# Scan loads and zero fills issued by ScalarE, delta writes by GpSimd, other buffer counts in the scan

## The chip, the cores and the metric

The kernel runs on one core of a Trainium2 chip. The metric is the time of one execution on the device in microseconds; a lower time is better. PE is the matrix engine (TensorE), PEld its weight loads, DVE VectorE, ACT ScalarE, POOL GpSimd, and SP is SyncE, which computes nothing and issues transfers (DMAs).

## The reference

Eight sequences (batches) of 512 steps with 256 channels pass through a chain with residual additions. Shortened to what the text below needs:

```
# 1. gated conditioning, then a Mamba layer
cond  = gated, causally averaged x (nine exponential averages), normalised
xc, z = split(cond @ W_in);  xc = silu(causal_conv4(xc) + conv_b)
dt, B, C = split(xc @ W_x);  delta = softplus(dt @ W_dt + b_dt);  A = -exp(A_raw)
h[t]  = exp(delta[t] * A) * h[t-1] + delta[t] * B[t] * xc[t]     # 16 states x 512 channels
y[t]  = sum_n C[t, n] * h[t, n] + D * xc[t]
x     = x + (y * silu(z)) @ W_out
# 2. per-batch linear layer, then 2 of 8 experts for each token (gelu), x = x + sum
# 3. per-batch low-rank feed-forward layer, then attention, 8 heads, 512 x 512 scores:
a     = softmax(q k^T);  x = x + sum over heads (a @ V)
# 4. per-batch bottleneck and layer norm, then 4 of 32 experts for each token, shared expert
```

## The kernel before

The work on the batches is written as two Python generators that are stepped in turn, so that their instructions lie mixed in the program. A scheduler then orders the instructions of each engine: it takes them by program order, but lets a later one that is ready pass an earlier one that is not. On the chip each engine works through its own queue in that order and stops at a wait.

**Thread X** (`thread_x`) does part 1 for batches 0 to 7. `head_a` computes the conditioning, with scans over time on DVE (line 479). `head_b` does the input projection, the convolution of four taps (lines 523 to 533: ACT writes the padded copy `xp` and the first tap, DVE adds three), silu, and delta (lines 557 to 574). What the scan needs goes through DRAM: `xzs` holds xc and silu(z), `packs` holds delta and delta * xc, because each block of 32 channels is read back repeated four times onto 128 partitions, one copy for each of four states. `scan` then works through 64 items (j, g, k) of a batch: j is a group of 128 channels, g a group of four states, k a block of 32 channels. `begin(i)` makes dA on ACT (line 623, the scaled Exp) and h on POOL (line 625); `run(i)` makes the recurrence on DVE (line 651) and the product with C (line 652); `add` sums over the states on PE (line 660), and adds D * xc on DVE (line 664) and multiplies with silu(z) on POOL (line 665). `begin` runs two items ahead of `run`. The same block `packed` serves the four g of a j, so a block is loaded (`get_pack`, line 595) for every four items, 128 times in all; its tiles are a ring of five, `dA` one of four, `h` one of eight. While batch b is scanned, the head of batch b+1 is stepped between the items; what is left of it is run before item 58.

**Thread Y** (`thread_y`) does parts 2 and 3 for groups of batches ([0], [1, 2], [3, 4, 5], [6, 7]) as soon as thread X has finished them: routing, scattering tokens into tables in DRAM (`tab`, `tok`) by indirect transfers of POOL (line 160), experts (loads `fw` and `xt`), then low-rank feed-forward and attention. In attention `scores` takes the maximum on DVE (line 893), Exp with its sum on ACT (line 896), the reciprocal on DVE (line 897) and the scaling with it on DVE (line 898); `turn` transposes on PE (line 906). Some copies out of PSUM are written with `nc.any`, and the scheduler gives them to ACT or DVE. Group [6, 7] runs when thread X is over, together with the routing of part 4; the 32 experts come last.

All plain transfers are issued by SP, in one queue for both threads; POOL issues only the indirect ones.

The tables have to be zero before tokens are scattered into them. `filling` steps thread X and, at every fourth of its pieces, issues one fill from a block of zeros, 56 in all of about 2 MB, and ties it to the DVE instruction written last (line 153):

```python
to, src = fills.pop(0)
tc.add_manual_dep(nc.sync.dma_start(to, src).ins, last_of(mybir.EngineType.DVE).name, SYNC)
```

Of the kernel before, what the change touches and what calls it, by code (L numbers as in the profile page):

```python
# [10 lines left out]
F32 = mybir.dt.float32  # L11
I32 = mybir.dt.int32
AF = mybir.ActivationFunctionType
ALU = mybir.AluOpType
# [3 lines left out]
P = 128  # L18
NB = 8
T = 512  # L20
# [31 lines left out]
def adaln_attn_ffn_kernel(ctx: ExitStack, tc: tile.TileContext, d: dict, out: bass.AP):  # L52
    nc = tc.nc
# [84 lines left out]
            fills.append((v[i], zeros[:, 0 : 16 * w]))  # L138
        return t

    def last_of(engine):
        return next(i for i in reversed(nc.cur_bb.bb.instructions) if i.engine == engine)

    def filling(pieces):

        first = E2 * len(GROUPS[0]) * T // (16 * P)
        z = const.tile([P, 132], F32, tag="z", name="z")
        nc.vector.memset(z, 0.0)
        nc.sync.dma_start(zeros.rearrange("p (r f) -> p r f", f=132), z[:, None, :].to_broadcast([P, 32, 132]))
        for n, c in enumerate(pieces):  # L150
            if fills and n % 4 == 1 and (n > 44 or n < 4 * first):
                to, src = fills.pop(0)
                tc.add_manual_dep(nc.sync.dma_start(to, src).ins, last_of(mybir.EngineType.DVE).name, SYNC)
            yield c

    members = {}
# [210 lines left out]
    def thread_x(wp, wk, ps):  # L367
# [63 lines left out]
                nc.vector.scalar_tensor_tensor(  # L431
                    cb[:, j : j + 1], wb[:, j : j + 1], col("convw", 4 * j + 3), col("convb", j), ALU.mult, ALU.add)

        xps = []
        for i in range(2):
            t = wp.tile([P, T + 3], F32, tag=f"xp{i}", name=f"xp{i}")
            nc.gpsimd.memset(t[:, 0:3], 0.0)
            xps.append(t)
        m3 = wp.tile([72, T], BF16, tag="m3", name="m3")
        nc.gpsimd.memset(m3, 0.0)  # L440

# [77 lines left out]
        def head_b(b):  # L519

            cn = rows[b]
            xc = wk.tile([P, 4, T], F32, tag="xc", name="xc")
            for j in range(4):
                pt = gx()
                mm(pt, [(W_in[:, k, ts(j, P)], cn[:, k, :]) for k in range(KC)])
                xp = xps[j % 2]
                nc.scalar.activation(xp[:, 3:], pt, AF.Identity, bias=wb[:, j : j + 1])
                cv = xc[:, j, :]
                nc.scalar.activation(cv, pt, AF.Identity, scale=col("convw", 4 * j + 3), bias=cb[:, j : j + 1])
                for i in range(3):  # L530
                    nc.vector.scalar_tensor_tensor(
                        cv, xp[:, i : i + T], col("convw", 4 * j + i), cv, ALU.mult, ALU.add)
                yield 3
            nc.scalar.activation(xc, xc, AF.Silu)
            nc.sync.dma_start(xzs[b % 2][:, :, 0, :], xc)
            for j in range(4):
                pt = gx()
                mm(pt, [(W_in[:, k, ts(4 + j, P)], cn[:, k, :]) for k in range(KC)])
                sz = wk.tile([P, T], F32, tag="sg", name="sz", bufs=2)
                nc.scalar.activation(sz, pt, AF.Silu, bias=wb[:, 4 + j : 5 + j])  # L540
                nc.sync.dma_start(xzs[b % 2][:, j, 1, :], sz)
            yield 5
            pt = gx()
            mm(pt[:96, :], [(W_x[:, j, :], xc[:, j, :]) for j in range(4)])
            dt = wk.tile([64, T], F32, tag="dt", name="dt")
            nc.scalar.copy(dt, pt[:64, :])
            bc3 = wk.tile([96, T], BF16, tag="bc3", name="bc3", bufs=2)
            split3(wk, pt[64:96, :], [bc3[64:96, :], bc3[32:64, :], bc3[0:32, :]], 64, 96)
            yield 3

            for j2 in range(2):
                dds, es = [], []
                for j in (2 * j2, 2 * j2 + 1):
                    pt = gx()
                    mm(pt, [(W_dt[:, ts(j, P)], dt)])

                    dd = wk.tile([P, 2, T], F32, tag=("gated", "ct")[j % 2], name="dd")
                    e = wk.tile([P, T], F32, tag="sg", name="sp_e", bufs=2)
                    nc.scalar.activation(e, pt, AF.Abs, bias=col("bdt", j))
                    nc.vector.tensor_scalar(dd[:, 0, :], pt, col("bdt", j), 0.0, ALU.add, ALU.max)  # L560
                    nc.scalar.activation(e, e, AF.Exp, scale=-1.0)
                    u = dd[:, 1, :]
                    nc.vector.tensor_scalar(u, e, 1.0, None, ALU.add)
                    nc.vector.scalar_tensor_tensor(e, u, 1.0, e, ALU.subtract, ALU.subtract)
                    dds.append(dd)
                    es.append(e)
                yield 3
                for dd in dds:
                    nc.scalar.activation(dd[:, 1, :], dd[:, 1, :], AF.Ln)
                for j, dd, e in zip((2 * j2, 2 * j2 + 1), dds, es):  # L570
                    u = dd[:, 1, :]
                    nc.gpsimd.tensor_tensor(u, u, e, ALU.subtract)
                    nc.gpsimd.tensor_tensor(dd[:, 0, :], dd[:, 0, :], u, ALU.add)
                    nc.gpsimd.tensor_tensor(dd[:, 1, :], dd[:, 0, :], xc[:, j, :], ALU.mult)
                    nc.sync.dma_start(packs[b % 2][j], dd)
                yield 3
            rows[b] = bc3

# [11 lines left out]

        def get_pack(b, j, k):

            t = wk.tile([P, 2, T], F32, tag="pack", name="packed", bufs=5)
            src = packs[b % 2][j, 32 * k : 32 * k + 32]
            nc.sync.dma_start(t, src[None].to_broadcast([4, 32, 2, T]))
            got[b, j, k] = t

        def get_B4(b, g):

            pt = gx()  # L600
            mm(pt, [(states(g), rows[b])])
            t = wk.tile([P, T], F32, tag="B4", name="B4", bufs=4)
            nc.scalar.copy(t, pt)
            B4s[b, g] = t
# [7 lines left out]
        def scan(b):  # L612
# [6 lines left out]
            def begin(i):  # L619
                j, g, k = items[i]  # L620
                t = got[b, j, k]
                dA = wk.tile([P, T], F32, tag="dA", name="dA", bufs=4)
                nc.scalar.activation(dA, t[:, 0, :], AF.Exp, scale=A[:, 4 * j + k, g : g + 1])  # L623
                h = wk.tile([P, T], F32, tag="h", name="h", bufs=8)
                nc.gpsimd.tensor_tensor(h, t[:, 1, :], B4s[b, g], ALU.mult)  # L625
                hs[i], dAs[i] = h, dA
                if (g, k) == (1, 0):
                    xz[j] = wk.tile([P, 2, T], F32, tag="xz", name="xz")
                    nc.sync.dma_start(xz[j], xzs[b % 2][:, j])
                if j == 0 and g < 3 and k == 1:  # L630
                    get_B4(b, g + 1)

                if j < 3 and (g, k) == (2, 3):
                    get_pack(b, j + 1, 0)
                if j < 3 and g == 3 and k < 3:
                    get_pack(b, j + 1, k + 1)
                if j == 3 and b + 1 < NB and g == 3:
                    if k == 0:
                        get_pack(b + 1, 0, 0)
                    if k < 3:  # L640
                        get_pack(b + 1, 0, k + 1)
                    if k == 3:
                        get_B4(b + 1, 0)

            def run(i):
                j, g, k = items[i]
# [20 lines left out]
            begin(0)  # L667
            begin(1)
            for i in range(64):
                if i == 58:  # L670
                    yield from after[0]
                if i < 62:
                    begin(i + 2)
                run(i)
                if i % 4 == 0 and i > 0:
                    add(i - 4)
                if i % 2:
                    yield 5
# [32 lines left out]
    def thread_y(q, bs, ps):  # L711
# [103 lines left out]
        with ExitStack() as ph:  # L815
            wk = ph.enter_context(tc.tile_pool(name=f"k3_{q}", bufs=1))
            H = 8
            for r, b in enumerate(bs):
# [43 lines left out]
                for hp in range(H // 2):  # L862
# [20 lines left out]
                    def scores(i):  # L883

                        sps = [g() for u in range(2)]

                        for u in (1, 0):
                            r0 = 64 * u
                            mm(sps[u], [(qk[r0 : r0 + 64, 0, ts(i, P)], qk[r0 : r0 + 64, 1, :])])
                        for u in range(2):  # L890
                            sp = sps[u]
                            nm = wk.tile([P, 1], F32, tag="nm", name="nm", bufs=4)
                            nc.vector.tensor_reduce(nm, sp, AX.X, ALU.max, negate=True)  # L893
                            ex = wk.tile([P, T], F32, tag="ex", name="ex", bufs=NEX)
                            den = wk.tile([P, 1], F32, tag="den", name="den", bufs=4)
                            nc.scalar.activation(ex, sp, AF.Exp, bias=nm, accum_out=den)  # L896
                            nc.vector.reciprocal(den, den)
                            nc.vector.tensor_scalar(ex, ex, den, None, ALU.mult)  # L898
                            exs[i, u] = ex

                    def turn(i):
# [300 lines left out]
```

## Time and profile before

| | before |
|---|---|
| median of 3 runs | 4261.57 us (4254.47 to 4265.86) |
| profiled execution | 4252.41 us, span from first to last instruction 4250.6 us |
| PE busy | 3440.5 us, 81% |
| DVE busy | 2670.9 us, 63% |
| ACT busy | 1672.2 us, 39% |
| POOL busy | 1565.8 us, 37% |
| transfers | 554.78 MB, mean 131 GB/s |
| granted PE clock, mean | 0.889 |

The profile is of one execution. Busy time counts no transfer issues. A line such as "POOL h L625 <- DMA packed<-pack: 190.2, 47, 16.1" says that POOL, ahead of the instruction of line 625 that writes h, sat idle until a transfer from `pack` into `packed` had landed: 190.2 us in total, 47 times, 16.1 us at the longest. SPq is the queue in which SP issues transfers. A line of the timeline has start, duration, engine, line and operation, and in brackets the idle time before it with what ended it. Shares over the whole span hide that the stages have different limits, so tables by stretch of time are used as well.

### The profile page before, as it was taken

The page shows a single profiled execution, that of the slowest core. Times are in us where ns is not written, and L with a number is a line of the kernel's source. Part 1 is how long each engine was busy: PE and PEld are TensorE (multiplying, and loading weights), DVE is VectorE, ACT ScalarE, POOL GpSimd, SP SyncE. Part 2 cuts the span into 40 slices and gives each one's busy share as a digit, 9 for nine tenths or more (in the row PEclk, how much of TensorE's full clock was granted, in tenths as well). Part 3 has the DMA queues.
Part 4 walks back from the last instruction along what each step waited for, and adds up shares of the span by engine and source line. Part 5 has one row for each costly group of instructions (what it writes and reads, how often), then busy time and mean ns, then how long its engine had stood idle before and what let it go on. Part 6 is the DMA issues. An engine that isn't in the chain of part 4 may idle for free. (4 is left out here: it accounts for less than half of the span.)

```text
span 4250.6 us, 36891 instructions
## 1 busy us (share of the span) xinstructions
PE 3440.5 (81%) x10964; PEld 1694.3 (40%) x10964; DVE 2670.9 (63%) x4290; ACT 1672.2 (39%) x2741; POOL 1565.8 (37%) x1222
## 2 busy tenths in 40 slices
PE   4556686887687888888758899889988999978994
PEld 2111352332254233333327443333456444436773
DVE  4698957886966686796892547575432454443336
ACT  2535463455366346445433443242223233322222
POOL 0456535434635333433542323231043111134552
PEclk7677798988798898999879999899989999989996
DMA  3235455324456423333346312213043312117776
GB/s 105 101 108 180 187 162 170 106 98 156 177 176 209 135 102 118 134 122 109 139 165 234 122 63 77 68 36 104 15 163 136 93 41 70 36 50 245 248 237 224
DMA packets 159372, 554.78 MB, mean 131 GB/s; under 512 B 27730, under 2 KB 34289, under 8 KB 146756
## 3 DMA queue, kind: packets, MB, share of 16 engines
q1 hardware_dynamic: 135076, 501.35, 35.2%
q0 software_dynamic: 24096, 51.08, 3.3%
q8 instruction: 87, 1.43, 0.1%
q14 instruction: 113, 0.93, 0.1%
HBM read 453.00 MB, written 234.82 MB: 162 GB/s over the span
## 5 line engine op out<-in xcount | busy, mean ns | idle before, releaser
L625 POOL TENSOR_TENSOR h<-packed,B 128x512 f32<-128x512 f32 x512 | 792.5, 1570 | 1054.2 <-PE yp L660 746.7
L651 DVE TENSOR_TENSOR_SCAN h<-dA,h 128x512 f32<-128x512 f32 x512 | 791.0, 1571 | 126.3 <-ACT dA L623 67.2
L623 ACT ACTIVATE dA<-packed,Aexp 128x512 f32<-128x512 f32 x512 | 359.8, 720 | 656.4 <-DVE h L651 446.5
L160 POOL DMA_INDIRECT tok<-ys,to_i x310 | 311.9, 1006 | 497.9 <-DVE ys L808 237.7
L660 PE MATMUL yp<-h,fold 128*32 128x512 f32 x1024 | 349.7, 704 | 156.9 <-DVE h L652 140.6
L923 PE MATMUL acc<-aT,V 128*128 128x512 f32 x1024 | 453.4, 597 | 5.3 <-ACT aT L907 3.2
L160 POOL DMA_INDIRECT tab<-row,si x192 | 197.4, 1028 | 465.5 <-issue 210.5
L652 DVE TENSOR_TENSOR h<-h,c 128x512 f32<-128x512 f32 x512 | 330.5, 672 | 29.0 <-PE c L78 28.2
L923 PEld LDWEIGHTS acc<-aT,V 128*128 128x128 f32 x1024 | 193.2, 191 | 245.9 <-issue 235.1
L78 PE MATMUL acc<-wv,c 128*128 128x512 f32 x512 | 270.2, 642 | 0.4
L78 PE MATMUL g<-qk 64*128 64x512 f32 x512 | 210.7, 681 | 54.9 <-ACT ex L896 28.6
L896 ACT ACTIVATE ex<-g,nm 128x512 f32<-128x512 f32 x256 | 173.8, 684 | 157.5 <-DVE nm L893 157.3
L78 PE MATMUL g<-xT,fw 128*128 128x256 f32 x960 | 233.6, 396 | 2.5 <-ACT h L801 1.9
L893 DVE TENSOR_REDUCE nm<-g 128x1 f32<-128x512 f32 x256 | 165.0, 681 | 100.8 <-PE g L78 100.8
L78 PE MATMUL acc<-fw,h 128*128 128x256 f32 x960 | 221.6, 383 | 3.5 <-DVE ys L808 1.8
L78 PEld LDWEIGHTS g<-xT,fw 128*128 128x128 f32 x960 | 188.0, 201 | 39.4 <-issue 6.8
L78 PEld LDWEIGHTS acc<-fw,h 128*128 128x128 f32 x960 | 182.7, 192 | 41.6 <-issue 12.4
L906 PE MATMUL acc<-ident,ex 128*128 128x128 f32 x1024 | 160.3, 286 | 47.9 <-DVE ex L898 16.2
L906 PEld LDWEIGHTS acc<-ident,ex 128*128 128x128 f32 x1024 | 122.6, 146 | 188.4 <-issue 69.3
L660 PEld LDWEIGHTS yp<-h,fold 128*32 128x32 f32 x1024 | 44.7, 115 | 364.1 <-DVE h L652 208.3
L479 DVE TENSOR_TENSOR_SCAN tr<-alpha,gm 128x512 f32<-128x512 f32 x128 | 181.4, 1435 | 5.0 <-POOL y L665 3.5
L78 PE MATMUL g<-xT,mw 128*128 128x256 f32 x760 | 183.1, 385 | 0.0
(280 smaller groups left out, 5458.3 us busy)
## 6 DMA issues: line engine op xcount, KB each, us to landing
fw<-in_fW SPq DMA_DIRECT2D x60, 1154.0 KB
tab<-zeros SPq DMA_DIRECT2D x32, 2112.0 KB
packed<-pack SPq DMA_DIRECT2D x128, 512.0 KB
mw<-in_mW SPq DMA_DIRECT2D x95, 384.0 KB
tab<-zeros SPq DMA_DIRECT2D x16, 2080.0 KB
xt<-tab SPq DMA_DIRECT2D x95, 264.0 KB
xz<-xzs SPq DMA_DIRECT2D x32, 512.0 KB
pack<-dd SPq DMA_DIRECT2D x32, 512.0 KB
```

Of the source, the lines that this page charges most:

```text
L78: nc.tensor.matmul(o, lhsT, rhs, start=(i == 0), stop=(i == len(pairs) - 1))
L160: i = nc.gpsimd.indirect_dma_start(out=table_, out_offset=bass.IndirectOffsetOnAxis(ap=idx, axis=0), in_=src, in_offset=None, bounds_check ...
L479: nc.vector.tensor_tensor_scan(tr, alpha[:, 1 + i : 2 + i].to_broadcast([P, T]), gm[:, k, :], 0.0, ALU.mult, ALU.add)
L623: nc.scalar.activation(dA, t[:, 0, :], AF.Exp, scale=A[:, 4 * j + k, g : g + 1])
L625: nc.gpsimd.tensor_tensor(h, t[:, 1, :], B4s[b, g], ALU.mult)
L651: nc.vector.tensor_tensor_scan(h, dAs.pop(i), h, 0.0, ALU.mult, ALU.add)
L652: nc.vector.tensor_tensor(h, h, Cs[0], ALU.mult)
L660: nc.tensor.matmul(yps[j][32 * k : 32 * k + 32, :], fold, hs.pop(i + k), start=(g == 0), stop=(g == 3))
L893: nc.vector.tensor_reduce(nm, sp, AX.X, ALU.max, negate=True)
L896: nc.scalar.activation(ex, sp, AF.Exp, bias=nm, accum_out=den)
L906: nc.tensor.transpose(tp[:, m, :], ex[:, ts(m, P)], ident)
L923: nc.tensor.matmul(ys[k], V[:, m, C * u + P * k : C * u + P * (k + 1)], aTs[u][:, m, :], start=(u == 0 and m == 0), stop=(u == 1 and m == 3))
```

## The change

Five things change together:

- The fills are issued by ScalarE, and the dependency on DVE's last instruction is gone.
- In thread X, the writes of xc and silu(z) to `xzs`, the loads of `xz` and the loads of the scan's blocks are issued by ScalarE; the writes of delta to `packs` by GpSimd.
- Six buffers for the blocks in place of five, three for `dA` in place of four, one padded copy `xp` in place of two. The loads of the next j are asked for at (g, k) = (2, 2), (2, 3), (3, 2) and (3, 3), before at (2, 3), (3, 0), (3, 1) and (3, 2).
- What is left of the next head is run before item 56 instead of 58.
- In attention the scaling of the exponentials is a ScalarE activation instead of a DVE operation.

```diff
-                tc.add_manual_dep(nc.sync.dma_start(to, src).ins, last_of(mybir.EngineType.DVE).name, SYNC)
+                nc.scalar.dma_start(to, src)
...
-        xps = []
-        for i in range(2):
-            t = wp.tile([P, T + 3], F32, tag=f"xp{i}", name=f"xp{i}")
-            nc.gpsimd.memset(t[:, 0:3], 0.0)
-            xps.append(t)
+        xp = wp.tile([P, T + 3], F32, tag="xp", name="xp")
+        nc.gpsimd.memset(xp[:, 0:3], 0.0)
...
-            nc.sync.dma_start(xzs[b % 2][:, :, 0, :], xc)
+            nc.scalar.dma_start(xzs[b % 2][:, :, 0, :], xc)
...
-                nc.sync.dma_start(xzs[b % 2][:, j, 1, :], sz)
+                nc.scalar.dma_start(xzs[b % 2][:, j, 1, :], sz)
...
-                    nc.sync.dma_start(packs[b % 2][j], dd)
+                    nc.gpsimd.dma_start(packs[b % 2][j], dd)
...
-            t = wk.tile([P, 2, T], F32, tag="pack", name="packed", bufs=5)
+            t = wk.tile([P, 2, T], F32, tag="pack", name="packed", bufs=6)
             src = packs[b % 2][j, 32 * k : 32 * k + 32]
-            nc.sync.dma_start(t, src[None].to_broadcast([4, 32, 2, T]))
+            nc.scalar.dma_start(t, src[None].to_broadcast([4, 32, 2, T]))
...
-                dA = wk.tile([P, T], F32, tag="dA", name="dA", bufs=4)
+                dA = wk.tile([P, T], F32, tag="dA", name="dA", bufs=3)
...
-                    nc.sync.dma_start(xz[j], xzs[b % 2][:, j])
+                    nc.scalar.dma_start(xz[j], xzs[b % 2][:, j])
...
-                if j < 3 and (g, k) == (2, 3):
-                    get_pack(b, j + 1, 0)
-                if j < 3 and g == 3 and k < 3:
-                    get_pack(b, j + 1, k + 1)
-                if j == 3 and b + 1 < NB and g == 3:
-                    if k == 0:
-                        get_pack(b + 1, 0, 0)
-                    if k < 3:
-                        get_pack(b + 1, 0, k + 1)
-                    if k == 3:
-                        get_B4(b + 1, 0)
+                if g == 2 and k > 1:
+                    block(j + 1, k - 2)
+                if g == 3 and k > 1:
+                    block(j + 1, k)
+                if j == 3 and g == 3 and k == 3 and b + 1 < NB:
+                    get_B4(b + 1, 0)
+
+            def block(j, k):
+                if j < 4:
+                    get_pack(b, j, k)
+                elif b + 1 < NB:
+                    get_pack(b + 1, 0, k)
...
-                if i == 58:
+                if i == 56:
                     yield from after[0]
...
-                            nc.vector.tensor_scalar(ex, ex, den, None, ALU.mult)
+                            nc.scalar.activation(ex, ex, AF.Identity, scale=den)
```

More of the change, by code (lines that the diff above doesn't have):

```diff
@@ L139, in table @@
         return t
-    def last_of(engine):
-        return next(i for i in reversed(nc.cur_bb.bb.instructions) if i.engine == engine)
     def filling(pieces):
@@ L525, in head_b @@
                 mm(pt, [(W_in[:, k, ts(j, P)], cn[:, k, :]) for k in range(KC)])
-                xp = xps[j % 2]
                 nc.scalar.activation(xp[:, 3:], pt, AF.Identity, bias=wb[:, j : j + 1])
```

## The prediction

> **What bounds the kernel now.** I read the stages first (busy time by stretch), then who waits for whom, then the waits of SP's transfer queue, and last the timeline of the start. Columns of the stages: length, busy us (instructions) of PE, PEld, DVE, ACT, POOL, then PE clock, transfer share, GB/s.
>
> ```profile
> 0.00:480.00 480.00, 273.29 (x515) 78.27 (x515) 360.04 (x409) 194.04 (x251) 217.89 (x149) 0.71 0.37 124
> 480.00:2950.00 2470.00, 2031.01 (x6239) 936.27 (x6239) 1747.43 (x2372) 1120.29 (x1789) 977.54 (x698) 0.90 0.39 132
> 2950.00:3810.00 860.00, 800.73 (x2617) 417.77 (x2616) 374.72 (x917) 249.19 (x479) 173.72 (x172) 0.96 0.23 78
> 3810.00:4180.00 370.00, 313.60 (x1532) 252.74 (x1530) 136.04 (x481) 92.42 (x191) 196.60 (x204) 0.96 0.70 222
> 4180.00:4250.00 70.00, 21.84 (x64) 9.26 (x64) 52.65 (x112) 16.27 (x32) 0.00 (x0) 0.50 0.81 300
> ```
>
> To 480 us only thread X runs (batch 0's head, its scan, batch 1's head); DVE is busy 75% and no thread-Y work covers a gap, so a stall there moves the end one for one. From 480 to 2950 X and Y share the engines: PE 82%, DVE 71%, neither full, both losing time to each other. After 2950 the scan is over and PE is 93% busy. The change can act before 2950, and on the softmax after it.
>
> ```profile
> POOL h L625 <- DMA packed<-pack: 190.2, 47, 16.1
> ACT dA L623 <- DMA packed<-pack: 132.2, 38, 7.7
> DVE h L651 <- ACT dA L623: 67.2, 19, 10.8
> DVE h L651 <- POOL h L625: 59.0, 22, 8.6
> DVE dd L560 <- DMA pack<-dd: 57.3, 11, 13.3
> PE acc L298 <- DMA xt<-tab: 39.8, 16, 9.0
> ```
>
> These are waits before 2950 us (total us, times, longest). GpSimd and ScalarE wait for scan blocks, but the cost shows only where DVE's scan then waits: 67.2 + 59.0 + 57.3 = 183.5 us, of which 41 before 500 (15.5 + 11.2 + 14.2 in that window) and 142 after. Why blocks come late is in SP's own waits:
>
> ```profile
> SPq L629 <- POOL y L665: 258.0, 22, 32.4
> SPq L575 <- POOL dd L574: 233.8, 31, 22.8
> SPq L595 <- ACT dA L623: 207.3, 37, 28.3
> SPq L595 <- POOL h L625: 149.5, 65, 23.9
> SPq L153 <- DVE h L652: 89.9, 11, 15.6
> SPq L785 <- DVE ys L808: 272.2, 32, 21.4
> ```
>
> One in-order queue issues X's and Y's transfers; each of these waits holds all behind it.
>
> [...] The trace has 0.32 to 0.56 us for an issue. [...] the trace has 0.72 for the scaled Exp of the same shape (L623).
>
> **The change, part by part.**
>
> *Fills, at the start: +40 us.* The manual dependency goes, and with it what held the 56 fills in place. In the changed program's order 17 fills stand on ScalarE before batch 0's first z write and 4 more before its first block load; before, 2 were issued in this time. [...] A fill is 2.16 MB; at the 300 GB/s of the last stage it takes 7.2 us. The start before:
>
> ```profile
> 28.00 10.21 SPq L153 DMA_DIRECT2D tab<-zeros  x2
> 115.24 0.62 SPq L535 DMA_DIRECT2D xzs<-xc  x1
> 119.84 0.32 SPq L629 DMA_DIRECT2D xz<-xzs  x1
> 119.88 0.58 ACT L546 COPY dt<-gx 64x512 f32<-64x512 f32 x1 [2.70 <-PE gx L78]
> 148.91 0.72 ACT L623 ACTIVATE dA<-packed,Aexp 128x512 f32<-128x512 f32 x1 [6.50 <-DMA packed<-pack]
> ```
>
> Worked forward: [...] Fills 4 to 8 drain by about 86 us under DVE's temporal scans (36 to 77 us), at no cost. Fills 9 to 17 are issued from about 84 to 118 us between Gelu, Sigmoid and convolution; nine at 7.2 us, one after another, end near 150. [...] the third z waits for the first z's landing (two buffers), the xz load for xc's, all near 152 to 155. The dt copy, 119.9 before, comes at about 157, and the first dA at about 188: +40, bounds +15 (fills overlap better) to +70 (block loads, behind fills 19 to 21, cost a full drain more).
>
> *Block loads and writes, 480 to 2950: -50 us.* 128 block loads, 32 xz loads, 40 xzs writes and 32 delta writes leave SP. Delta writes follow GpSimd's own last product. Six buffers let two of the next four loads go six to eight scan steps ahead; the other two wait for slots freed two steps before. I take two thirds of the 142 us as caused by late blocks and writes (a choice: all of dd's 43, some half of the waits for dA and h, whose other cause is ScalarE or GpSimd busy elsewhere), 95, and half of that as end-time, since PE and DVE alternate as the bound: -50, bounds 0 to -142. *The same before 500:* 27 of 41, all exposed: -25, bounds 0 to -41; batch 0's scan then meets fewer fills.
>
> *Y's loads with SP freed: -15.* PE waits 39.8 us for xt; half could go with X's waits off that queue, less what fw's own wait for ys still holds. Bounds 0 to -40.
>
> *Softmax: -15.* 256 scalings of 0.632 (161.8 us) leave DVE; 256 of about 0.72 (184) come to ScalarE. The scheduler answers: 123 any-engine copies (aT 79, V 32, qk 12) go from ScalarE (0.58, -72 us) to DVE (0.68, +84). Net DVE -78, ScalarE +113, less four table loads of 1.28. After 2950 (96 of 256) PE's 93% hides both: 0. Before (160 of 256) DVE sheds 49 us, a third of it on the path: -15, bounds +15 (ScalarE now waits for the reciprocal ahead of the next Exp) to -45.
>
> *ScalarE's new duties: +25.* 128 x 0.54 + 32 x 0.33 + 40 x 0.54 + 56 x 0.56 = 133 us of issue, about 105 between 480 and 2950. With +67 of softmax its load there goes from 1120 to about 1290 of 2470 us: cover is left. But three decay buffers let it lead DVE by one step less, a single xp makes each convolution step wait for DVE's three multiply-adds (3 x 0.83 us), and the xz load waits for GpSimd's y (SP stood 258 us there). Behind each stand dA for DVE and Y's evictions. I take a fifth of 133; bounds 0 to +140. GpSimd's 32 issues at about 1.0 us (the indirect writes, L160) fall in its 60% idle time: 0, to +10.
>
> Sum: +40 - 50 - 25 - 15 - 15 + 25 = -40. The profiled execution took 4252.4 us (span 4250.6): 4212. The median of the runs is 9 above it: **4221**.
>
> **The rivals.**
> - *The stalls pay in full.* The 95 us count whole and xt gives 30: +40 - 95 - 25 - 30 - 15 + 25 = -100, 4161. For it: PE idles 439 us between 480 and 2950, and stretches near 1100 and 2100 where DVE alone binds. Against: a shorter DVE wait often only shifts to PE.
> - *ScalarE becomes the bottleneck of order (slower).* Place: its queue inside the scan, where some 200 transfer issues after the start wait for GpSimd[...] or slots, with dA behind them and only three buffers. Charging 0.7 us of DVE stall to each makes 140 instead of 25: +75, 4336. It decides from about 0.4 us each (78 us): slower by 0.3%. For it: dA already waits 446 us for freed buffers, so the lead is used up. Against: issue is about 0.5 us, a step about 5.5.
> - *Hidden anyway:* late blocks are a symptom of DVE's order, gains reach only 50, and the start eats them: 4250 to 4275.
> - *It does not do what it says:* fills are no longer paced, they only stand where the scheduler finds ScalarE free; this is in the first term.
>
> **How the numbers follow.** A measurement of this kernel can tell about 0.3% (13 us). Chances: my sum 0.45 (own range 4175 to 4258), stalls in full 0.18, hidden 0.10, ScalarE slower 0.27. Faster 0.60, same 0.13, slower 0.27. The range 4120 to 4325 leaves out the far ends of the second case and of the fourth.
>
> **What would show it.** Right: first dA near 188 us; idle of GpSimd and ScalarE on packed down from 322 to under 150; DVE's wait for pack writes near 0; PE 2950 to 3810 as before. Wrong: first dA under 165 (the first term falls); dA as the releaser of the scan at over 150 us (the third case's queue); PE idle on xt unchanged; the end of X later than 2920.

## The result: slower by 2.8%

The changed kernel takes 4382.19 us (median of 4 runs, 4364.06 to 4387.75) against 4258.68 for the kernel before on the same chip: +123.5 us, a ratio of 1.0281 with a 95% interval of 1.0247 to 1.0315. The profiled execution has a span of 4383.0 us.

Stages of the kernel after, in the columns of the stages shown before:

```profile
0.00:480.00 480.00, 243.74 (x427) 64.51 (x427) 299.57 (x319) 167.27 (x217) 184.15 (x133) 0.72 0.55 182
480.00:2950.00 2470.00, 2011.80 (x6036) 907.20 (x6035) 1723.29 (x2320) 1161.47 (x1826) 1006.88 (x732) 0.89 0.35 118
2950.00:3810.00 860.00, 801.91 (x2577) 410.81 (x2578) 341.64 (x788) 280.74 (x532) 157.53 (x150) 0.96 0.24 79
```

In the first 480 us DVE does 60 us less work than before and PE 30 us less: thread X is late from the start. X's result of batch 0 is written (`xa<-xr`) at 469.6 us, before at 406.4; that of batch 3 at 1511.1 (1411.6); that of batch 7, the end of X, at 3023.8 (2938.5). The first output leaves at 4324.1 (4192.4). So 63 us are lost by the end of batch 0, 85 by the end of X, and some 46 more after it.

The waits of the compute engines up to 3030 us, kernel after (total us, times, longest):

```profile
DVE to_m L303 <- DMA xt<-tab: 177.9, 25, 12.8
POOL h L618 <- DMA packed<-pack: 126.8, 26, 16.2
PE acc L295 <- DMA xt<-tab: 62.5, 20, 9.8
DVE h L645 <- ACT dA L616: 60.2, 19, 10.0
DVE dd L553 <- DMA pack<-dd: 50.3, 6, 18.1
DVE h L645 <- POOL h L618: 34.7, 19, 9.1
ACT dA L616 <- DMA packed<-pack: 30.2, 12, 5.5
```

GpSimd and ScalarE wait 157 us for scan blocks (before 322), as the change makes one expect. But DVE's three waits in the scan only went from 183.5 to 145.2 us, and the waits for thread Y's `xt`, which the change doesn't touch, rose: PE from 39.8 to 62.5, DVE's `to_m` from 84.2 to 177.9. Of SP's own waits those for X's moved transfers are gone. Three of the rest, over the whole span:

```profile
SPq L860 <- PE acc L78: 665.3, 27, 49.7
SPq L779 <- DVE ys L802: 424.8, 44, 22.9
SPq L922 <- DMA packed<-pack: 142.3, 2, 94.6
```

SP now stands at Y's loads, whose buffers PE and DVE free late (lines 860 and 779: 376.6 and 355.6 before). In the last line, line 922 writes `xb` and has no use for a scan block, yet SP stood there until one had landed. With five more lines, SP waits 229.4 us for block loads and xzs writes of ScalarE that its own transfers don't use; before, when SP issued both, such waits were 3.4 us. What ties these transfers to each other the traces don't show.

The start, in ScalarE's timeline:

```profile
145.82 0.69 ACT L533 ACTIVATE sz<-gx,wb 128x512 f32<-128x512 f32 x1 [23.51 <-DMA xzs<-sz]
152.46 0.58 ACT L539 COPY dt<-gx 64x512 f32<-64x512 f32 x1 [2.39 <-PE gx L78]
181.70 1.28 ACT L554 ACT_TABLE_LOAD   x1 [16.22 <-issue]
190.13 0.72 ACT L616 ACTIVATE dA<-packed,Aexp 128x512 f32<-128x512 f32 x1 [1.03 <-DMA packed<-pack]
```

The first dA comes at 190.13, before at 148.91. In the scan ScalarE meets a wait that it did not have before:

```profile
ACT dA L616 <- POOL y L659: 26.4, 6, 10.5
```

### The profile page after: what moved, and what is told of

The parts are those of the page before. It is cut to its first block, busy times and chain, and to the rows that moved or that the text cites. A ratio compares the mean times of both kernels' runs of the same rounds, so it can differ in the third digit from the quotient of the medians.

```text
span 4383.0 us, 36642 instructions
## 1 busy us (share of the span) xinstructions
PE 3506.2 (80%) x10964; PEld 1697.5 (39%) x10964; DVE 2611.3 (60%) x4157; ACT 1761.7 (40%) x2870; POOL 1581.8 (36%) x1253
## 4 chain that ended last, share of the span: by engine, by line
PE 36%; DVE 23%; issue 15%; DMA 10%; POOL 9%; ACT 5%; another core or an unknown queue 1%; SPq 1%; ACTq 0%; POOLq 0%; DVEq 0%
PE g L78 12%; PE acc L917 8%; DVE h L645 8%; PE gx L78 5%; PE acc L78 4%; POOL tok L157 4%; DVE tr L473 3%; DMA xt<-tab 3%; DVE h L646 3%; PE acc L848 2%; PE yp L654 2%; DMA packed<-pack 2%; PE acc L900 2%; DMA tg<-tok 2%; POOL h L618 2%
## 5 line engine op out<-in xcount | busy, mean ns | idle before, releaser
L618 POOL TENSOR_TENSOR h<-packed,B 128x512 f32<-128x512 f32 x512 | 782.3, 1552 | 998.1 <-PE yp L654 629.7
L645 DVE TENSOR_TENSOR_SCAN h<-dA,h 128x512 f32<-128x512 f32 x512 | 796.1, 1578 | 95.4 <-ACT dA L616 60.2
L654 PE MATMUL yp<-h,fold 128*32 128x512 f32 x1024 | 416.3, 715 | 162.8 <-DVE h L646 141.6
L892 ACT ACTIVATE ex<-ex,den 128x512 f32<-128x512 f32 x256 | 177.0, 720 | 75.8 <-DVE den L891 72.0
L303 DVE SCALAR_TENSOR_TENSOR to_m<-xt,sc_teb 128x8 f32<-128x8 f32 (+1 forms) x155 | 36.2, 234 | 272.5 <-DMA xt<-tab 272.1
L921 DVE TENSOR_TENSOR x<-x,acc 128x512 f32<-128x512 f32 x64 | 43.6, 683 | 249.1 <-PE acc L917 243.0
```

Of the source, the lines that this page charges most:

```text
L645: nc.vector.tensor_tensor_scan(h, dAs.pop(i), h, 0.0, ALU.mult, ALU.add)
L654: nc.tensor.matmul(yps[j][32 * k : 32 * k + 32, :], fold, hs.pop(i + k), start=(g == 0), stop=(g == 3))
L892: nc.scalar.activation(ex, ex, AF.Identity, scale=den)
```

## The experiments

Each difference is the median against that of the kernel before on the same chip, with the ratio's 95% interval. "xa" is the time of batch 7's write, the end of X, in the profile (2938 before).

### Parts alone, and parts undone

**e1_fills_alone**: the kernel before with the fills moved and untied.

```diff
-                tc.add_manual_dep(nc.sync.dma_start(to, src).ins, last_of(mybir.EngineType.DVE).name, SYNC)
+                nc.scalar.dma_start(to, src)
```

> The kernel before with one part of the change: the fills are issued by ScalarE and lose their dependency. Theory A (the unpaced fills at the start are the larger part of the loss): first dA near 190 us, end of batch 0 some 50 to 65 us later than 406, and the time 40 to 80 above before (4300 to 4340). Theory B (fills cost the start only, gained back by a freer SP queue): first dA near 190, time within 20 of before. Theory C (the loss comes from the block loads on ScalarE or the softmax, not from fills): first dA later, but time at most 20 above before.

Measured: +151 us (1.0315 to 1.0376), more than the whole change and above all three forecasts. First dA at 191.6, so 43 us belong to the start; end of X 3078.

**e2_fills_back**: the changed kernel with the diff of e1 undone.

> The changed kernel with the fills back on SP, tied to DVE's last instruction as before. Theory A: first dA back near 150 us and the time 40 to 80 below the changed kernel, 4300 to 4340. Theory C: first dA back, but the time at most 30 below the changed kernel, since what was lost in the scan stays lost. If the time falls below before (4259), the rest of the change is a gain hidden by the fills.

Measured: +88 us (1.0155 to 1.0212). Without the fills' move seven tenths of the loss are still there, between what theories A and C gave. The parts don't add.

**e3_softmax_back** and **e4_softmax_alone**: the scaling back on DVE in the changed kernel, and the scaling on ScalarE alone in the kernel before.

```diff
-                            nc.vector.tensor_scalar(ex, ex, den, None, ALU.mult)
+                            nc.scalar.activation(ex, ex, AF.Identity, scale=den)
```

> The changed kernel with the scaling of the exponentials back on DVE. Theory D (ScalarE waits for DVE's reciprocal ahead of the next Exp, and attention gets longer): 25 to 50 below the changed kernel, the stretches of the last two batches' attention back from 246 and 239 us to about 238 and 224. Theory E (the scaling is neutral where PE binds and relieves DVE elsewhere, as in my prediction): 0 to 20 above the changed kernel.

> The kernel before with one part of the change: exponentials scaled on ScalarE. Theory D: 25 to 50 above before (4285 to 4310). Theory E: 0 to 20 below before.

Measured: e3 +128 us (1.0248 to 1.0306), not told apart from the changed kernel. e4 +21 us (1.0031 to 1.0057), outside both of its forecasts. In e4 X ends at 2939, 1 us from before: what it loses, it loses in the stage after X, where I had put 0. (Its profile has 43 us there; that execution lies 9 us above its median, and the profiled one of before 13 us below the median that e4 is compared with.)

**e5_fills_tied**: the kernel before, fills on ScalarE and tied as they were. **e8_after_tied**: the same tie in the changed kernel.

```diff
-                tc.add_manual_dep(nc.sync.dma_start(to, src).ins, last_of(mybir.EngineType.DVE).name, SYNC)
+                tc.add_manual_dep(nc.scalar.dma_start(to, src).ins, last_of(mybir.EngineType.DVE).name, SYNC)
```

> The kernel before with the fills issued by ScalarE but still tied to DVE's last instruction. It splits the 151 us that fills alone cost. Theory A1 (they cost because nothing holds them back): within 20 of before, first dA near 150 us. Theory A2 (they cost because ScalarE issues them, waits and all): 60 to 150 above before.

> The changed kernel with its fills on ScalarE tied to DVE's last instruction. If pacing is what matters: near the changed kernel with fills back on SP (4353), so 20 to 40 below the changed kernel. If ScalarE as issuer matters: near the changed kernel, 4382. Below 4320: SP loses more by fills than ScalarE does.

Measured: e5 +138 us (1.0314 to 1.0356), e8 +120 us (1.0259 to 1.033). In e5 the first dA is at 145.4, so the way to it costs nothing, and the end of X is 3068 all the same. The pacing sets where the loss falls, and hardly how large it is.

**e6_queues_alone**: the kernel before with the block's loads, xz's loads and xc's and sz's writes on ScalarE and delta's writes on GpSimd, as in the change.

> The kernel before with one part of the change: block, xz and z transfers issued by ScalarE and delta's writes by GpSimd; fills, buffers and softmax as before. My prediction's own account: 50 to 90 below before, idle of GpSimd and ScalarE on packed from 322 to under 200. Theory Q (ScalarE's order suffers, and SP gets waits of another kind): 20 to 80 above before.

Measured: +133 us (1.0293 to 1.0413), above both forecasts; end of X 3070. The idle time on packed rises to 445 us between 190 and 3030 (302.6 before).

**e7_buffers_alone**: six block buffers, three dA, one xp, the other places of the loads, item 56.

> The kernel before with one part of the change: six block buffers, three decay buffers, one padded copy, the loads asked for at the new places, the head finished before item 56. Theory B (fewer decay buffers and a single padded copy hurt): 20 to 60 above before, with dA as releaser of the scan above 67 us. Theory B0 (neutral or a small gain from the sixth buffer): 20 below to 10 above.

Measured: +5 us (1.0000 to 1.0022). Its waits up to 2960 us:

```profile
POOL h L621 <- DMA packed<-pack: 90.3, 23, 15.9
DVE h L648 <- ACT dA L619: 52.5, 19, 10.5
DVE h L648 <- POOL h L621: 51.3, 20, 8.5
ACT dA L619 <- DMA packed<-pack: 37.5, 8, 12.0
DVE dd L556 <- DMA pack<-dd: 29.5, 8, 8.5
```

The idle time on blocks is cut from 322 to 128 us by the buffers alone, and the kernel gains nothing. DVE's own three waits fall too, from 183.5 to 133.3 us, and that gains nothing either: the 50 us went into other waits. (The order of the work was free in e7; that a gain by the buffers and a loss by another order cancel there is not ruled out.)

### Which property of the moved transfers costs

After these runs I held that a second issuer, ScalarE, costs by itself: through its queue, or by SP's waits for ScalarE's transfers (229.4 us in the changed kernel). Four kernels, all from the kernel before: fills on GpSimd (e9), delta's writes alone on GpSimd (e10), small transfers on ScalarE beside the fills (e11), only xc's and sz's writes on ScalarE (e12).

```diff
# e9
+                tc.add_manual_dep(nc.gpsimd.dma_start(to, src).ins, last_of(mybir.EngineType.DVE).name, SYNC)
# e10
+                    nc.gpsimd.dma_start(packs[b % 2][j], dd)
# e11, beside the fill on SP
+                tc.add_manual_dep(nc.scalar.dma_start(tiny[n : n + 1], zeros[0:1, 0:128]).ins, last_of(mybir.EngineType.DVE).name, SYNC)
# e12
+            nc.scalar.dma_start(xzs[b % 2][:, :, 0, :], xc)
+                nc.scalar.dma_start(xzs[b % 2][:, j, 1, :], sz)
```

> The kernel before with its 56 zero fills, tied to VectorE's work as they were, issued by GpSimd. [...] ScalarE issues nothing. Theory A (ScalarE as issuer[...] makes the loss of +138 us): 0 to +40 us, fills that hold GpSimd's own additions of the block up a little; the idle time on packed stays near 322 us. Theory B (any move of the fills off SP costs[...]): +100 to +150 us, and the idle time on packed near 400 us.

> The kernel before with delta's 32 writes alone issued by GpSimd; loads, xz's and the fills stay on SP. Theory A (the loss of +133 us with the block's queues moved is ScalarE's part): -15 to +20 us. Theory B (a write through GpSimd lands later and the loads of a block wait for it): +30 us or more, with more idle time on packed.

> The kernel before, fills on SP, and beside each fill one transfer of 512 bytes to scratch that nothing reads, issued by ScalarE and tied to VectorE's work in the same way. It adds 56 issues on ScalarE and no traffic worth the name. Theory A1 (a second issuer itself costs: its instructions stand in ScalarE's queue[...]): +80 to +150 us. Theory B (it is the 2 MB beside the loads): within 15 us of before.

> The kernel before with the 40 writes of xc and sz (what ScalarE itself has just made) issued by ScalarE; everything else stays on SP. ScalarE then waits for no other engine's data before these issues. Theory A2 (the loss is ScalarE standing at issues that wait for data, with its evictions and decays queued behind): -10 to +20 us. Theory A1 [...]: +40 to +130 us, with SP waiting for transfers that it does not use, such as a fill or an x load behind xzs<-sz.

Measured: e9 +130 us (1.0289 to 1.0324), e10 +55 us (1.0118 to 1.0173), e11 +23 us (1.0033 to 1.0066), e12 +27 us (1.0048 to 1.0082). e9 ends my theory: ScalarE issues nothing there, and the loss is nearly as large as with ScalarE. e11 is above the 15 us of its theory B and far below the 80 of A1, which speaks against a second issuer as the main cause. e12 lies between its two forecasts and decides nothing. e10 is above its 30 us, but its idle time on packed is as before (302.8 us between 190 and 3030), so not for the reason given there; what its 55 us are stays open.

What e1, e5, e6 and e9 have in common is that SP is relieved. The scheduler lets ready instructions pass others, so with another load on SP it makes another order for all engines: in e5's program 1998 of PE's 6584 instructions and 1426 of DVE's 4092 stand in another place of their engine's queue than before. (In e10 it is 831 of PE's, in e12 1415.) That is a cause which none of the runs so far could tell from the transfers themselves.

### The order held, and the order alone

So the order was made an experiment of its own. At the end of the program an edge that fixes the order of issue, and waits for nothing, is laid between each two instructions that follow one another on PE, DVE, ACT, POOL and SP in a stored order. The moved transfers and the copies written with `nc.any` stay free, so some copies still go to another engine: of those of aT, V and qk, DVE makes 146 in p5, 145 in p6, and 121 in p9 as in the kernel before.

```diff
+def hold(tc):
+    nc = tc.nc
+    traced = list(nc.cur_bb.bb.instructions)
+    for code in ORDER:                 # one stored order for each engine
...
+        row = [i for i in row if i.engine == row[0].engine]
+        for one, two in zip(row, row[1:]):
+            tc.add_manual_dep(two, one.name, NOSYNC)
```

> Fills tied and issued by ScalarE, but every other instruction of TensorE, VectorE, ScalarE, GpSimd and SyncE held in the order it has in the kernel before (without that hold the same move cost +138 us). Theory O (the order of the engines' work, remade when SP is relieved, is what costs): -20 to +35 us. Theory C [...]: +90 to +150 us.

> Fills issued by GpSimd, all other work held in the order of the kernel before (without the hold +130 us). Theory O: -20 to +35 us. Theory C: +90 to +150 us.

> The block's loads and xz's transfers on ScalarE and delta's writes on GpSimd, fills on SP, all other work held in the order of the kernel before (without the hold +133 us). Theory O: -30 to +40 us. Theory C: +90 to +150 us.

> The kernel before, every transfer on the engine that it had, fills on SP and tied; only the order of the engines' work is held as it came out when ScalarE issued the fills. Theory O: +90 to +150 us, most of it gone by the end of X. Theory C: -20 to +30 us.

| what is moved | order remade | order of before held |
|---|---|---|
| fills to ScalarE, tied | e5 +138 | p5 +57 (1.0100 to 1.0158) |
| fills to GpSimd | e9 +130 | p9 +25 (1.0040 to 1.0081) |
| loads to ScalarE, delta to GpSimd | e6 +133 | p6 +98 (1.0191 to 1.0257) |
| nothing | r5, with the order of e5: +107 (1.0226 to 1.0267) | the kernel before itself |

For the fills the order is the larger part: it costs 107 us where no transfer is moved, and with the old order the moves cost 25 and 57. (The two don't add: 107 and 57 are more than e5's 138.) For the loads it is not: 98 of 133 us stay. So p9 fits theory O, and p6 theory C, that the moved transfers cost with the old order too; p5 lies between, and neither theory is right for both moves. PE's waits before and then in r5, over the whole span:

```profile
PE yp L660 <- DVE h L652: 140.6, 47, 7.5
PE yp L673 <- DVE h L665: 205.8, 71, 27.7
PE acc L311 <- DMA xt<-tab: 67.8, 23, 9.1
```

Line 673 is line 660 of the kernel before: in r5 PE stands longer at the sum over the states. In the changed kernel this wait is 141.6 us, so it is not what the order costs there. DVE, before and then in r5:

```profile
DVE to_m L306 <- DMA xt<-tab: 178.4, 32, 14.8
DVE to_m L319 <- DMA xt<-tab: 262.2, 38, 14.6
```

It is 272.1 us in the changed kernel, and 158 to 191 in p5, p9, p6 and h_all (below). DVE's longer wait for `xt` is a mark of the new order, and not of the fills beside the loads.

With the order held, p6 has waits of ScalarE that the kernel before has not:

```profile
ACT dA L636 <- POOL y L678: 68.2, 12, 10.6
ACT cen L518 <- POOL y L678: 17.5, 2, 8.8
```

None of these instructions reads y. ScalarE stands at the xz load ahead of them, whose buffer GpSimd's y still holds: 104.5 us with four more such lines. Before, SP stood there (258.0 us), with no arithmetic behind it. That these 104.5 us make the 98 is not shown: DVE's scan waits for dA about as long as before (60.2 us, before 67.2), so some of the standing only takes the place of other idle time. Two rivals are in the same trace: the idle time on packed is 377.7 us between 190 and 3030 (302.6 before), and SP waits 126.4 us, in eight lines of its waits, for transfers that ScalarE issued.

The last two divide the change itself. **h_all_held** makes all moves of the change but its buffers, with the old order held (DVE makes 241 of the free copies there, 244 in the changed kernel); **r_all_order** is the kernel before with the order that these moves bring.

> All of the change's moves (fills untied on ScalarE, the block's and xz's transfers on ScalarE, delta's writes on GpSimd, the scaling of the exponentials on ScalarE) but its buffers, with all other work held in the order of the kernel before. If the order is most of the change's +124 us: +20 to +60 us. If ScalarE's and GpSimd's new duties are most of it, as the +98 us of the loads alone suggests: +90 to +170 us, the parts adding (startup +41, loads' queue +98, attention +21).

> The kernel before, every transfer and scaling on the engine that it had; only the order of the engines' work is held as these moves bring it out. If the order is most of the loss: +80 to +140 us. If the duties are: -20 to +50 us.

Measured: h_all +95 us (1.0195 to 1.0268), r_all +164 us (1.0357 to 1.0419). The moves lose without the new order, within the second forecast of h_all. The new order loses without the moves, and more than was forecast. 95 and 164 are not shares of 123.5: the new order was made for the new queues and is worse on the old ones. With the new queues it takes the loss from 95 to about 124 us (the buffers, near zero alone, included); the intervals of h_all and of the changed kernel overlap, so this last step is hardly clear of noise.

In h_all the first dA is at 182.65, 34 us late, and X ends 101 us late; from there to the first output nothing more is lost (+91). ScalarE stands behind y for 91 us (60.8 ahead of dA), and GpSimd's wait for ScalarE's `s_m` grows from 146.9 to 197.0 us. Late blocks are not its loss: the idle time on packed is 205.7 us, below the kernel before. In the changed kernel ScalarE stands behind y for only 42 us.

### The stage after X

The stretch from the end of X to the last write of `xb`, in the kernels before, e4, after and h_all, in this order:

```profile
2938.00:3761.00 823.00, 778.14 (x2565) 406.52 (x2564) 356.69 (x872) 242.89 (x471) 161.93 (x161) 0.97 0.24 81
```
```profile
2939.00:3807.00 868.00, 813.44 (x2628) 419.89 (x2627) 328.54 (x804) 289.92 (x546) 164.91 (x163) 0.96 0.23 79
```
```profile
3024.00:3899.00 875.00, 816.04 (x2628) 421.67 (x2627) 328.98 (x804) 289.91 (x546) 165.04 (x163) 0.96 0.23 78
```
```profile
3040.00:3857.00 817.00, 773.31 (x2564) 403.43 (x2564) 327.49 (x801) 288.01 (x541) 162.44 (x162) 0.97 0.24 82
```

In e4 and in the changed kernel PE has 64 matmuls more in this stage and is about as full as before, so the stage is 45 to 52 us longer. Groups of PE in it, before and then e4, say which:

```profile
L854 PE MATMUL acc<-hi,wo 128*128 128x512 f32 x74 | 36.5, 615 | 0.7 <-ACT hi L851 0.7
L78 PE MATMUL g<-x,wi 128*128 128x512 f32 x72 | 35.0, 606 | 1.4 <-DVE wi L838 0.8 <-DVE x L822 0.6
```
```profile
L854 PE MATMUL acc<-hi,wo 128*128 128x512 f32 x96 | 47.4, 616 | 0.0
L78 PE MATMUL g<-x,wi 128*128 128x512 f32 x95 | 46.0, 605 | 0.7 <-DVE x L822 0.7
```

It is low-rank feed-forward, some 24 matmuls more of each of these kinds, which before was done ahead of the end of X. With the scaling on ScalarE and the order held (h_all) it is back in its old place, and ScalarE's 288 us of work in this stage cost nothing. It comes with the order that the scheduler makes for the scaling on ScalarE, and not with every new order: r_all, scaling on DVE, has about 64 matmuls more in this stage too, and r5 none.

## Why the prediction was wrong

The forecast was 4221 us and a gain; the range to 4325 did not hold 4382. Three of its terms (block loads and writes, Y's loads, ScalarE's new duties) were to give -65 us together. The moves of these transfers cost +133 us (e6), and +98 with the order of the work held (p6). That is where the prediction failed, and it would have failed without the new order too: h_all, with the order held, loses 95 us where the sum had a gain of 40.

- **Fills at the start, +40: right in its place, and in part by luck in its figure.** The first dA was forecast near 188 and came at 190.13, with the third z waiting 23.51 us for the first z's landing, which came 26.7 us after its issue. From 85 to 182 us the DMA engines are busy 0.91 to 0.96, at 306 to 325 GB/s. That the fills drain one after another, with the writes behind them, was my estimate, and the trace does not show it. But the dt copy came at 152.46 for a forecast 157, and the 16.22 us that ScalarE then stood at an issue were not in the working: the two errors nearly cancel.
- **Block loads and writes, -75: the step that fails is "half of that as end-time".** The idle time on blocks fell about as forecast (322 to 157, forecast under 150). e7 shows what that is worth: by buffers alone it fell to 128 us, and DVE's waits by 50, for +5 us. As far as e7 goes, the rival "hidden anyway" was right on this term. DVE's wait for pack writes, forecast near zero, is 50.3 us (57.3 before), with the writes on GpSimd's queue. Of the 25 us to be gained before 500 nothing is seen: batch 0 ends 63 us late with its first dA 41 late, so its scan lost some 22 more.
- **Y's loads with SP freed, -15: not there.** It took SP's queue as what makes `xt` late. With SP freed and the order held PE waits for `xt` as long as before (p6, 52.4 us over the whole span, before 48.2). DVE's wait for `xt` follows the order of the work: r5 has it long (262.2 us) with SP as it was, p6 short (190.5) with SP freed.
- **Softmax: 0 after 2950, right with the order held, wrong in the kernel as it is.** The forecast counted the copies that the scheduler would move between engines, but took the place of everything else as given. e4 lost 21 us, after X; the 15 us to be gained before are not there either, since its X ends as before. In the whole change taking it back gains nothing (e3).
- **ScalarE's new duties, +25: the term was mis-sized.** "A fifth of 133" charges issue time. What p6 shows beside it is the time that an issue stands waiting for other engines' data, 104.5 us behind y alone, and a loss of 98 us. The rival "ScalarE becomes the bottleneck of order" had named this place, a transfer that waits with dA behind it, and its total, 75 us above before, is the nearest of all the cases to h_all's 95. But its mark, DVE waiting over 150 us for dA, is not there (60.2): the loss shows in other waits, such as those for `s_m`, and how much of it comes from standing behind y was not isolated.
- **A term is missing:** the order of the engines remade when a queue is relieved. It is worth 107 us alone for the fills. On top of the moves in this change it is about 29 us, hardly clear of noise.

The sign of being wrong that came true is the end of X later than 2920: it was 3024. One reading was off, at no cost to the sum: thread Y works before 480 us, since its linear layer for batch 0 begins at 428 (PE, `g<-x,cw`).

Open: h_all loses some 68 us in the scan beyond its start. How they divide between ScalarE standing at issues, SP waiting for ScalarE's transfers that it doesn't use (161.9 us in h_all), and transfers that would land later while fills are under way was not isolated. What single place in the new order costs the 107 us of r5 is open too.

## What to carry to other kernels

In a program that a scheduler orders, a transfer moved to another queue can be two changes, the transfer and the order of everything else; hold the order and try each alone before explaining either. Before moving an issue, look at the wait that its old queue stood at it (258 us on SP for xz) and at what would stand behind it in the new queue, and not only at its issue time. An idle time that shrinks is worth only what the end of the kernel then gains: try it by the cheapest part of the change alone, here the buffers.

## What the runs showed of the hardware

With the order of the other work held, the same 56 fills cost 25 us from GpSimd and 57 from ScalarE; 25 copies more on DVE are part of the second figure. An issue of a delta write takes GpSimd 0.6 us (605 ns in e10, where the forecast had 1.0 from the indirect writes), and an issue of a block load takes ScalarE 0.52 us (median in the changed kernel).
